# Feed-forward: the output of the second chunk of a half goes in front of the fourth chunk's first layer and the second GELU pair

## The chip, the cores and the metric

The kernel runs on one core of one Trainium2 chip. The time is the device time of one execution in microseconds (us). A core has five engines with an instruction queue each: TensorE (PE, matrix products; its weight loads are shown as PEld), VectorE (DVE), ScalarE (ACT), GpSimd (POOL) and SyncE (SP, which issues transfers). Engines meet through semaphores, and each works through its own queue strictly in order.

## The reference

The input x has the shape (2, 1024, 288), 16 heads of 18. Four layers follow each other. Layers 0 and 1 are quantised transformer blocks; in short:

```python
h = layer_norm(x, ln1_g, ln1_b, 1e-06)
q8, s, sm = quant_act(h)                      # per token: max|h|/127, round, row sum
q, k, v = (quant_linear(q8, s, sm, w, b) for (w, b) in ...)
a8, sa, sma = quant_act(attn(q, k, v))
x = x + quant_linear(a8, sa, sma, wo1, bo1)   # self-attention, 1024 x 1024
...                                           # cross-attention to 154 context tokens, the same way
h = layer_norm(x, ln3_g, ln3_b, 1e-05)
q8, s, sm = quant_act(h)
h = quant_linear(q8, s, sm, wfc1, bfc1)       # 288 -> 1152
h = jax.nn.gelu(h, approximate=False)
q8, s, sm = quant_act(h)
return x + quant_linear(q8, s, sm, wfc2, bfc2)   # 1152 -> 288
```

`quant_act` scales each token by its largest absolute value to integers of at most 127; `quant_linear` multiplies integers by quantised weights and scales back. Layers 2 and 3 are plain cross-attentions to the context, split into 86 text tokens and 68 others, each with its own softmax, without feed-forward. The change touches only the feed-forward, the last block shown.

## The kernel before

x stays in SBUF as 16 chunks of 128 tokens, eight for each of the two batch elements. The work is written as Python generators. `self_attention` is the main one: it runs over four self-attentions (layer 0, batch 0 and 1; layer 1, batch 0 and 1). Beside it, `beside(main, n_main, side, n_side, by)` advances "side" generators in proportion: preparation of weights, the cross-attention and feed-forward of the batch element whose self-attention has ended (`rest`), and the preparation of the next self-attention. So the feed-forward of layer 0, batch 0 runs beside the self-attention of layer 0, batch 1, and so on; the last one, of layer 1, batch 1, runs beside `plain_layers`, layers 2 and 3.

The whole kernel is one block of the Tile scheduler (L53, `schedule_with_timeline_sim=True`). Each engine gets a fixed list of instructions at compile time. The order comes from the order of the program and from a planner's own model of when each instruction would be ready; buffers come from pools with a fixed number of slots, and an instruction that needs a slot waits until its last reader is done. A moved line can therefore change the order of neighbouring work too, of the self-attention as well.

`feed_forward(w, b, name)` (L1313) works in two halves of four chunks; with two layers and two batch elements there are eight halves, called h1 to h8 in order of time. Each half begins with `ln_quantise` (LayerNorm: statistics on DVE L409, normalisation on ACT L422, eight multiplies and adds with gain and bias on POOL L430, then quantisation) and `transposed`. Then a table of (function, chunk) is worked through, and after each entry but `gelu` the generator yields to the main work. The functions are:

- `linear(c)`: the first layer, four times three matmuls (L456, tile `cf`) and a scaling on DVE (L467) into the float tile `ch`, 1152 wide. `ch` has three slots.
- `gelu(c)`: GELU on ACT, in place, for chunk c+1 (L1339) and then chunk c (L1340), tied together by `follow`, so that one load of ACT's function table serves both. The exponentials of the attention (L662) need another table, so a change between the two shows as a table load.
- `integers(c)`: quantises `ch` to the integers `cg`: largest value (DVE L373), scale and reciprocal (DVE L374, L375), small columns on POOL (L1345, L380 to L383), scaling on DVE (L385), rounding with row sum on ACT (L389), two small steps on DVE (L399, L400).
- `output(c)`: two groups of five PE transposes (L1355, `cpt`), each copied by ACT (L1358, `cgT`); ten matmuls (L1361, `co`); a scaling on DVE (L1369, `cu`); the add to x on POOL (L472).

The transposes, the first layer and the output share the two PSUM slots of `mm` (L148). What is called T, O and F with a chunk's number in this text are its transposes, its output matmuls and its first layer. Where a half runs alone it is called bare (h2, h4, h8 around the change); in the others attention work stands between its instructions. Other tiles met below: `aats`, `aatse`, `aato` are scores, exponentials and products of the self-attention (L660, L662, L674), `atse` the same exponentials in the plain layers; `amx` and `amxh` (L600, L607) the search for the largest scores, and `amxsr` (L581) its results on their way.

Of the kernel before, what the change touches and what calls it, by code (L numbers as in the profile page):

```python
# [53 lines left out]
def tile_xattn(ctx: ExitStack, tc: tile.TileContext, ins: dict, out: bass.AP):  # L54
# [56 lines left out]
    def follow(one, other):  # L111

        one, other = (getattr(i, "ins", i) for i in (one, other))
        tc.add_manual_dep(
            one,
            other.name,
            mybir.DependencyInfo(
                mybir.DependencyClass.NoSync, mybir.DependencyReason.DATA
            ),
            reason="kept together",  # L120
        )
# [17 lines left out]
    def big(name):  # L139
        return work.tile([P, FF], F32, tag="big", name=name, bufs=3)  # L140

    def bf(name):
        return work.tile([P, 3 * HQ], BF16, tag="bf", name=name, bufs=3)
# [4 lines left out]
    def mm(name, dtype=F32):  # L148
        n = 512 if dtype == F32 else 1024
        return ps_m.tile([P, n], dtype, tag="mm", name=name)  # L150
# [4 lines left out]
    def view(ap, **kw):  # L155
        names = list(kw)
        return ap.rearrange(f"p ({' '.join(names)}) -> p {' '.join(names)}", **kw)
# [246 lines left out]
    def ln_quantise(c0, ln, eps, s, name, h=None, q=None, eng=nc.gpsimd):  # L404
        st = small.tile([P, HC, 6], F32, tag="bn", name=f"{name}st")
        mv = small.tile([P, HC, 2], F32, tag="mv", name=f"{name}mv")
        rstd = small.tile([P, HC], F32, tag="rstd", name=f"{name}r")
        for c in range(HC):
            nc.vector.bn_stats(st[:, c, :], x[:, c0 + c, :])  # L409
            nc.vector.bn_aggr(mv[:, c, :], st[:, c, :])  # L410
        nc.vector.tensor_scalar(
            rstd, mv[:, :, 1:2].rearrange("p c a -> p (c a)"), eps, None, ALU.add
        )
        nc.gpsimd.tensor_tensor(rstd, rstd, neghalf, ALU.pow)
        shift = small.tile([P, HC], F32, tag="shift", name=f"{name}sh")
        nc.vector.scalar_tensor_tensor(
            shift.unsqueeze(2), mv[:, :, 0:1], -1.0, rstd.unsqueeze(2), ALU.mult, ALU.mult
        )
        if h is None:
            h = view(big(f"{name}h"), c=HC, w=C)  # L420
        for c in range(HC):
            nc.scalar.activation(  # L422
                h[:, c, :],
                x[:, c0 + c, :],
                AF.Identity,
                bias=shift[:, c : c + 1],
                scale=rstd[:, c : c + 1],
            )
            for j, op in ((0, ALU.mult), (1, ALU.add)):
                eng.tensor_tensor(h[:, c, :], h[:, c, :], ln[:, j, :], op)  # L430
        if q is None:
            q = bf(f"{name}q")
        q = view(q[:, 0 : HC * CZ], c=HC, w=CZ)
        quantise(h, q, s, HC, C, f"{name}qs")
        return q

    def transposed(q, name, qT=None):

        if qT is None:
            qT = bf(f"{name}qT")  # L440
        qT = view(qT[:KZ], k=3, t=HQ)
        for c0 in range(0, HC, 2):
            ptv = view(mm(f"{name}pt", BF16)[:KZ, 0 : 6 * P], k=3, t=2 * P)
            for c in range(2):
                for k in range(3):
                    nc.tensor.transpose(
                        ptv[:, k, c * P : (c + 1) * P],
                        q[:, c0 + c, k * KZ : (k + 1) * KZ],
                        ident16,
                    )  # L450
            nc.scalar.copy(qT[:, :, c0 * P : (c0 + 2) * P], ptv)
        return qT
# [5 lines left out]
    def quant_linear(qT, c, w, s, dst, name, shape=lambda ap: ap):  # L458

        qw, row = w  # L460
        ps = mm(name)[:, 0:C]
        matmul3(
            ps,
            lambda k: qT[:, k, c * P : (c + 1) * P],
            lambda k: qw[:, k, :, :],
        )
        nc.vector.scalar_tensor_tensor(  # L467
            dst, shape(ps), s, shape(row), ALU.mult, ALU.mult
        )

    def add_to_x(n, t):
        nc.gpsimd.tensor_tensor(x[:, n, :], x[:, n, :], t, ALU.add)  # L472

    def tmp(name):
        return work.tile([P, C], F32, tag="tmp", name=name, bufs=3)
# [837 lines left out]
    def feed_forward(w, b, name):  # L1313

        qw2, row2 = w["2"]
        for hf in range(2):
            c0 = b * 8 + hf * HC
            s1 = small.tile([P, HC], F32, tag="st", name=f"{name}st")
            q = ln_quantise(c0, w["ln"], 1e-5, s1, f"{name}l")
            yield 8  # L1320
            qT = transposed(q, f"{name}t")
            yield 2
            hs, gs = {}, {}

            def linear(c):
                hs[c] = big(f"{name}h")
                for j, wj in enumerate(w["1"]):
                    quant_linear(
                        qT,
                        c,  # L1330
                        wj,
                        s1[:, c : c + 1],
                        hs[c][:, j * C : (j + 1) * C],
                        f"{name}f",
                    )

            def gelu(c):

                a = nc.scalar.activation(hs[c + 1], hs[c + 1], AF.Gelu)  # L1339
                follow(nc.scalar.activation(hs[c], hs[c], AF.Gelu), a)  # L1340

            def integers(c):
                s = small.tile([P, HC], F32, tag="s", name=f"{name}s")[:, 0:1]
                g = bf(f"{name}g")[:, 0:FZ]
                nc.gpsimd.memset(g[:, FF + NZ : FZ], 0.0)  # L1345
                quantise(hs[c].unsqueeze(1), g.unsqueeze(1), s, 1, FF, f"{name}qs")
                gs[c] = g, s

            def output(c):
                g, s = gs[c]  # L1350
                gT = view(bf(f"{name}gT")[:KF, 0 : 10 * P], k=10, t=P)
                for k0 in (0, 5):
                    ptv = view(mm(f"{name}pt", BF16)[:KF, 0 : 5 * P], k=5, t=P)
                    for k in range(5):
                        nc.tensor.transpose(  # L1355
                            ptv[:, k, :], g[:, (k0 + k) * KF : (k0 + k + 1) * KF], ident16
                        )
                    nc.scalar.copy(gT[:, k0 : k0 + 5, :], ptv)  # L1358
                ps = mm(f"{name}o")[:, 0:C]
                for k in range(10):  # L1360
                    nc.tensor.matmul(  # L1361
                        ps,
                        lhsT=gT[:, k, :],
                        rhs=qw2[:, k, :],
                        start=(k == 0),
                        stop=(k == 9),
                    )
                t = tmp(f"{name}u")
                nc.vector.scalar_tensor_tensor(t, ps, s, row2, ALU.mult, ALU.mult)  # L1369
                add_to_x(c0 + c, t)  # L1370


            for f, c in (
                (linear, 0),
                (linear, 1),
                (gelu, 0),
                (integers, 0),
                (linear, 2),
                (output, 0),
                (integers, 1),  # L1380
                (linear, 3),
                (gelu, 2),
                (output, 1),
                (integers, 2),
                (integers, 3),
                (output, 2),
                (output, 3),
            ):
                f(c)
                if f is not gelu:  # L1390
                    yield 2
# [253 lines left out]
    def rest(n, b, *between):  # L1645
        pre = (L0, L1)[n]
        return chain(
            cross_attention(wb[n], b, f"{pre}b"),
            *between,
            feed_forward(wc[n], b, f"{pre}c"),  # L1650
        )
# [102 lines left out]
```

## Time and profile before

| what | value |
|---|---|
| time, median of three runs (lowest, highest) | 2461.59 us (2456.64, 2463.33) |
| the profiled execution | 2467.29 us, span 2465.5 us |
| granted TensorE clock, mean | 0.871 of full speed |
| busy share: PE, DVE, ACT, POOL | 79%, 72%, 60%, 39% |

The eight halves were found in the trace by their tiles. The page's line of 40 slices for PE and for its clock shows the course:

```profile
PE   2579988888777878887679678877777888778888
PEclk9689999899787989998789689986887988878999
```

One slice is 61.6 us. A digit is the busy share, or the granted clock, in tenths. The feed-forward halves lie around 656 to 767, 1118 to 1231, 1645 to 1755 and 2088 to 2206 us, so in the eleventh to thirteenth slice, the nineteenth and twentieth, the twenty-seventh to twenty-ninth and the thirty-fourth to thirty-sixth (counted from 1): the places with 7, 6 and 7 again belong to them or border on them. In a timeline row the first two numbers are start and length in us, then come engine, line, operation, the tile written and those read, the shape, the number of instructions joined in the row, and in brackets how long the engine had been idle and what released it.

### The profile page before, as it was taken

What the parts mean: (1) busy time and instruction counts of PE and PEld (TensorE: products, weight loads), DVE (VectorE), ACT (ScalarE), POOL (GpSimd) and SP (SyncE); (2) the same over time, 40 slices, a digit from 0 to 9 for tenths busy, and PEclk for the clock granted to TensorE, in tenths of its full rate; (3) what the DMA queues carried; (4) which work ended last, traced back from release to release, by engine and by line L of the source; (5) the groups of instructions that cost most, each with busy time, mean ns of one, the idle gap of its engine ahead of it and who ended that gap; (6) DMA issues with size and microseconds to landing.
All of it is one profiled execution on the core that took longest, in us unless ns stands there. A gap on an engine that the chain in (4) does not pass through costs nothing. (4 is left out here: it accounts for less than half of the span.)

```text
span 2465.5 us, 33556 instructions
## 1 busy us (share of the span) xinstructions
PE 1941.7 (79%) x10524; PEld 852.0 (35%) x10524; DVE 1777.5 (72%) x4213; ACT 1475.3 (60%) x2897; POOL 973.6 (39%) x2038
## 2 busy tenths in 40 slices
PE   2579988888777878887679678877777888778888
PEld 1223333332233243323333243323334443444444
DVE  6699997699775758997469848883255785745666
ACT  3257767675577667756676357756555665554443
POOL 4334224551325455432353545523247562313320
PEclk9689999899787989998789689986887988878999
DMA  3523212221001322100032031100123311112321
GB/s 76 169 69 98 68 40 65 69 64 42 9 1 52 108 76 61 48 24 13 12 101 79 23 90 47 38 9 12 35 73 92 86 55 31 50 38 74 85 79 38
DMA packets 160003, 141.58 MB, mean 57 GB/s; under 512 B 44123, under 2 KB 156339, under 8 KB 159760
## 3 DMA queue, kind: packets, MB, share of 16 engines
q1 hardware_dynamic: 148656, 121.90, 17.0%
q0 software_dynamic: 3584, 12.04, 2.0%
q10 hardware_dynamic: 7584, 5.47, 1.2%
q8 instruction: 84, 1.38, 0.2%
q14 instruction: 95, 0.78, 0.1%
HBM read 96.60 MB, written 39.37 MB: 55 GB/s over the span
## 5 line engine op out<-in xcount | busy, mean ns | idle before, releaser
L662 ACT ACTIVATE L_xattn_aatse<-L_xattn_aats 128x512 f32<-128x512 f32 x1024 | 575.9, 597 | 267.5 <-PE L_xattn_aats L660 253.0
L607 DVE TENSOR_REDUCE L_xattn_amxh<-L_xattn_amx 128x1 f32<-128x512 f32 x1024 | 658.5, 680 | 71.6 <-PE L_xattn_amx L600 68.7
L660 PE MATMUL L_xattn_aats<-L_xattn_aqT,kT 120*128 120x512 bf16 x1024 | 389.3, 406 | 88.8 <-ACT L_xattn_aatse L662 46.5
L600 PE MATMUL L_xattn_amx<-kT,L_xattn_aqT 108*128 108x512 bf16 x1024 | 388.1, 414 | 65.5 <-DVE L_xattn_amxh L607 40.3
L674 PE MATMUL L_xattn_aato<-L_xattn_aatse,L_xattn_av 128*32 128x512 f32 x2048 | 297.7, 652 | 43.5 <-ACT L_xattn_aatse L662 40.1
L641 POOL TENSOR_TENSOR L_xattn_bmxm<-L_xattn_bmxm,L_xattn_bm 128x308 f32<-128x308 f32 x256 | 199.7, 785 | 161.1 <-ACT L_xattn_bmxm L640 152.4
L662 ACT ACTIVATE L_xattn_atse<-L_xattn_ats 86x512 f32<-86x512 f32 (+1 forms) x256 | 142.2, 590 | 118.3 <-PE L_xattn_ats L660 99.7
L660 PEld LDWEIGHTS <-kT 120*128 120x128 bf16 x1024 | 96.2, 101 | 329.6 <-issue 292.1
L600 PEld LDWEIGHTS <-L_xattn_aqT 108*128 108x128 bf16 x1024 | 102.7, 103 | 216.3 <-issue 162.3
L646 DVE TENSOR_REDUCE L_xattn_mxn<-L_xattn_mx 128x2 f32<-128x172 f32 (+1 forms) x512 | 124.6, 303 | 39.2 <-PE L_xattn_mx L630 38.4
L640 ACT COPY L_xattn_bmxm<-L_xattn_bmx 128x308 f32<-128x308 f32 x256 | 104.0, 416 | 69.4 <-DVE L_xattn_bmxn L646 30.1
L646 DVE TENSOR_REDUCE L_xattn_bmxn<-L_xattn_bmxm 128x2 f32<-128x308 f32 x256 | 116.5, 460 | 25.2 <-POOL L_xattn_bmxm L641 24.9
L747 ACT ACTIVATE L_xattn_batse<-L_xattn_batse 128x512 f32<-128x512 f32 x160 | 100.2, 630 | 41.4 <-DVE L_xattn_batse L746 37.9
L660 PE MATMUL L_xattn_ats<-L_xattn_qT,L_xattn_kT 120*86 120x512 bf16 (+1 forms) x256 | 100.1, 422 | 29.9 <-ACT L_xattn_atse L662 15.5
L746 DVE TENSOR_TENSOR L_xattn_batse<-L_xattn_bats,L_xattn_bmT 128x512 f32<-128x512 f32 x160 | 107.7, 681 | 21.3 <-PE L_xattn_bats L752 8.0
L1495 PE MATMUL L_xattn_o<-wo,L_xattn_p 128*128 128x288 f32 x320 | 99.9, 455 | 9.6 <-DVE L_xattn_p L819 9.3
L674 PEld LDWEIGHTS L_xattn_aato<-L_xattn_aatse,L_xattn_av 128*32 128x32 f32 x2048 | 42.3, 111 | 172.3 <-ACT L_xattn_aatse L662 143.2
L630 PE MATMUL L_xattn_bmx<-L_xattn_bkT,L_xattn_bqT 108*128 108x154 bf16 x512 | 73.8, 245 | 23.8 <-DMA L_xattn_bqT<-L_xattn_bqr 8.8
L630 PE MATMUL L_xattn_mx<-L_xattn_kT,L_xattn_qT 108*128 108x154 bf16 x512 | 71.5, 257 | 22.3 <-DMA L_xattn_qT<-L_xattn_r 7.5
L1361 PE MATMUL L_xattn_co<-L_xattn_wfc2t,L_xattn_cgT 117*128 117x288 bf16 x320 | 65.9, 360 | 26.8 <-ACT L_xattn_cgT L1358 25.4
L674 PE MATMUL L_xattn_ato<-L_xattn_atse,L_xattn_v 68*32 68x512 f32 (+1 forms) x512 | 77.4, 677 | 8.1 <-DVE L_xattn_atT L847 4.3
L1495 PEld LDWEIGHTS L_xattn_o<-wo,L_xattn_p 128*128 128x128 f32 x320 | 65.9, 214 | 34.2 <-DVE L_xattn_p L819 14.8
(632 smaller groups left out, 3768.0 us busy)
## 6 DMA issues: line engine op xcount, KB each, us to landing
kT<-L_xattn_akr SPq DMA_DIRECT2D x192, 72.0 KB
L_xattn_aqT<-L_xattn_aqr SPq DMA_DIRECT2D x192, 72.0 KB
L_xattn_bqT<-L_xattn_bqr SPq DMA_DIRECT2D x192, 72.0 KB
L_xattn_qT<-L_xattn_r SPq DMA_DIRECT2D x192, 72.0 KB
L_xattn_akr<-L_xattn_akst SPq DMA_DIRECT2D x16, 324.0 KB
L_xattn_aqr<-L_xattn_aqst SPq DMA_DIRECT2D x16, 324.0 KB
L_xattn_bqr<-L_xattn_bqst SPq DMA_DIRECT2D x16, 324.0 KB
L_xattn_r<-L_xattn_qst SPq DMA_DIRECT2D x16, 324.0 KB
```

The lines of the kernel that those rows point to most:

```text
L600: nc.tensor.matmul(sp, lhsT=qt[:KR, j, c * P : (c + 1) * P], rhs=kt[:KR, j, a * 512 : (a + 1) * 512], start=True, stop=True,)
L607: nc.vector.tensor_reduce(halves[:, a, c, j, :], sp, AX.X, ALU.max, negate=True)
L630: nc.tensor.matmul(sp[:, j * T : (j + 1) * T], lhsT=qt[:KR, 2 * a + j, c * P : (c + 1) * P], rhs=kt[:KR, 4 * g + 2 * a + j, 0:T], start=Tr ...
L640: nc.scalar.copy(lm, of)
L641: nc.gpsimd.tensor_tensor(lm, lm, mask[:, c : c + 1, 0:T].to_broadcast([P, 2, T]), ALU.add)
L646: nc.vector.tensor_reduce(nm[:, c, 2 * a : 2 * a + 2, n], of[:, :, k0:k1], AX.X, ALU.max, negate=True,)
L660: nc.tensor.matmul(sp, lhsT=keys(j), rhs=qt[:KM, j, :], start=True, stop=True)
L662: nc.scalar.activation(e, sp, AF.Exp)
L674: made = nc.tensor.matmul(po[32 * i : 32 * i + 32, :], lhsT=lhsT, rhs=rhs, start=start, stop=stop)
L746: nc.vector.tensor_tensor(e, sp, maskT[:, m, :], ALU.add)
L747: nc.scalar.activation(e, e, AF.Exp)
L1495: nc.tensor.matmul(ps, lhsT=t[:, c * P : (c + 1) * P], rhs=wo[:, u0 + u, :], start=(u == 0), stop=(u == len(tiles) - 1),)
```

## The change

One entry of the table in `feed_forward` moves up by two places. The output of chunk 1 (its transposes, copies, matmuls, scaling and add to x) is handed to the scheduler directly behind the integers of chunk 1, and so in front of chunk 3's first layer and of the GELU of chunks 3 and 2; before, it came behind both. The generator yields at the same number of places; one yield that came behind chunk 1's output now comes before chunk 3's first layer. No instruction is added or taken away in the program, no buffer changes.

```diff
@@ -1378,9 +1378,9 @@
                 (linear, 2),
                 (output, 0),
                 (integers, 1),
+                (output, 1),
                 (linear, 3),
                 (gelu, 2),
-                (output, 1),
                 (integers, 2),
                 (integers, 3),
                 (output, 2),
```

In the compiled lists of instructions the change shows in all eight halves, and around them in the order of attention work too: the lists of the engines are the same up to about 680 us of the old time line and from about 2190 us on. The lists of PE, DVE, POOL and SP hold the same instructions as before in another order; that of ACT holds two table loads fewer.

## The prediction

> **What bounds the kernel now.** I read the page's busy shares first, then the eight stretches in which a feed-forward half runs, then the timeline of one half, then the list of waits. (1) Over the whole span no engine is full: PE 79%, DVE 72%.
>
> ```profile
> PE 1941.7 (79%) x10524; PEld 852.0 (35%) x10524; DVE 1777.5 (72%) x4213; ACT 1475.3 (60%) x2897; POOL 973.6 (39%) x2038
> ```
>
> (2) Windows: us, then the busy time of PE, weight load, DVE, ACT and POOL, then the granted clock. In order: a stretch between feed-forwards, the second halves of layer 0's two batch elements (h2, h4), and the first half of layer 1 (h5).
>
> ```profile
> 830.00:900.00 70.00, 58.16 (x324) 24.54 (x324) 56.22 (x130) 45.88 (x106) 32.42 (x68) 0.93 0.23 64
> 720.00:767.00 47.00, 29.77 (x190) 16.52 (x188) 26.02 (x66) 31.76 (x52) 16.33 (x37) 0.78 0.03 8
> 1190.00:1231.00 41.00, 22.56 (x133) 12.71 (x131) 21.27 (x54) 25.94 (x42) 14.29 (x34) 0.71 0.05 14
> 1645.00:1702.00 57.00, 42.57 (x238) 19.21 (x235) 28.13 (x66) 40.60 (x67) 23.48 (x60) 0.73 0.05 12
> ```
>
> PE falls from 83% to 63% and 55%: in these halves a chain bounds, which hops from engine to engine. (3) The chain of h2, from the timeline (start, length, engine, line, tiles, in brackets the idle time before and its releaser):
>
> ```profile
> 738.23 1.32 PE L1355 MATMUL L_xattn_cpt<-ident,L_xattn_cg 128*117 128x128 bf16 x10 [1.95 <-ACT L_xattn_cg L389]
> 739.85 2.58 PE L1361 MATMUL L_xattn_co<-L_xattn_wfc2t,L_xattn_cgT 117*128 117x288 bf16 x10 [0.31 <-ACT L_xattn_cgT L1358]
> 745.39 0.52 DVE L467 SCALAR_TENSOR_TENSOR L_xattn_ch<-L_xattn_cf,L_xattn_cst,L_xattn_wfc_864row 128x288 f32<-128x288 f32 x1
> 745.79 0.69 ACT L1358 COPY L_xattn_cgT<-L_xattn_cpt 117x640 bf16<-117x640 bf16 x1 [1.95 <-PE L_xattn_cpt L1355]
> 746.50 1.28 ACT L1339 ACT_TABLE_LOAD   x1
> 746.54 0.79 PE L1361 MATMUL L_xattn_co<-L_xattn_wfc2t,L_xattn_cgT 117*128 117x288 bf16 x5
> 747.80 1.16 ACT L1339 ACTIVATE L_xattn_ch<-L_xattn_ch 128x1152 f32<-128x1152 f32 x1
> 750.05 2.61 DVE L373 TENSOR_REDUCE L_xattn_cqs<-L_xattn_ch 128x1 f32<-128x1152 f32 x2 [4.13 <-ACT L_xattn_ch L1340]
> 750.65 1.38 PE L1361 MATMUL L_xattn_co<-L_xattn_wfc2t,L_xattn_cgT 117*128 117x288 bf16 x5 [3.32 <-ACT L_xattn_cgT L1358]
> 753.84 0.51 DVE L1369 SCALAR_TENSOR_TENSOR L_xattn_cu<-L_xattn_co,L_xattn_cs,L_xattn_wfc2row 128x288 f32<-128x288 f32 x1
> 757.26 1.52 PE L1355 MATMUL L_xattn_cpt<-ident,L_xattn_cg 128*117 128x128 bf16 x10 [5.24 <-ACT L_xattn_cg L389]
> ```
>
> The reader is to see two things. After chunk 3's first layer the half is one chain: GELU pair, two reduces, scale, rounding, transposes of chunk 2 at 757.26. And chunk 1's output (745.32 to 752.03 on PE) lies inside that chain's shadow: PE waits 3.32 us in it, and then 5.24 us more, and nobody needs it.
>
> **The change, part by part.** The order of instructions shows the same work on PE, DVE, POOL and the queues; ACT loses two table loads. In all eight halves ten transposes (T1), two copies, ten matmuls (O1), the scaling `cu` on DVE and the add to x on POOL move in front of chunk 3's first layer (F3) and the GELU pair.
>
> *T1 and O1 ahead of F3.* They leave their cover and F3 comes later by what they take on PE. Lower bound, all rows at the full clock: 0.44+0.44 transposes, 0.69 copy (the second beside it), 0.79+0.79 matmuls = 3.15. Upper bound, chunk 0's own pass: 742.43−738.23 = 4.20. I take 3.4, nearer the first, since PE's row there is warm (granted 0.88 from 742.2 to 746). F3 itself took 742.43 to 745.91 = 3.48, bound by its DVE rows. So in h2 F3's end goes to 742.43+3.4+3.48 = 749.3. Cheaper than 3.4, because before GELU waited for the load and for chunk 1's first copy: it began at 747.80, 1.9 us behind F3. Now the table is held in h2, and GELU begins at 749.3: **+1.5**. In h4 and h8 (GELU at 1211.90 and 2184.63 before) the same sum gives +1.4 and +1.5, if the load is early there too.
>
> *What comes back.* `cu` leaves the DVE chain between reduces and scale: −0.42 in h2 (753.84 to the next row at 754.26), −0.43 and a 0.44 statistics step in h4, −0.48 in h8 (2189.47 to 2189.95). Bare halves: h2 +1.1, h4 +0.5, h8 +1.1.
>
> *Mixed halves (h1, h3, h5, h6, h7), where a self- or cross-attention shares the engines.* GELU moves by +2.6 (h1, h3), +3.3 (h5), +2.8 (h6), +2.1 (h7): F3's delay of 3.4 less what GELU waited for its load. In h7 the attention's exponentials stand behind the pair:
>
> ```profile
> 2121.88 1.28 ACT L1339 ACT_TABLE_LOAD   x1
> 2123.17 1.16 ACT L1339 ACTIVATE L_xattn_ch<-L_xattn_ch 128x1152 f32<-128x1152 f32 x1
> 2127.53 1.28 ACT L662 ACT_TABLE_LOAD   x1 [1.68 <-issue]
> 2128.82 1.08 ACT L662 ACTIVATE L_xattn_atse<-L_xattn_ats 86x512 f32<-86x512 f32 x2
> ```
>
> so both streams are late: +2.0. In h1 and h3 the exponentials lose 0.4, the rounding 1.6: +1.5 each. In h5 POOL's casts, not GELU, release chunk 3's last transpose (1.79 us of PE at 1691.59), and the Wq and Wk issues and 13 casts of L106 (0.27 us each) now run ahead of them: +1.0. In h6 +0.9. Bounds: 0 if the attention's work fills every delay, the GELU shift itself if it fills nothing; I take the values given, because exponentials wait in the same ACT queue.
>
> *Table loads.* One pair fewer: three exponentials go ahead of h2's first pair. They cost 1.1 of ACT less in h2's front and are charged in h1's end: −1.1. The rows price a load at 1.28, GELU starting 0.02 behind; the pair is 2.57, already in the +1.5 of h2 (one) and hidden in ACT's free 32% of h2 (the other). [...]
>
> *Waits that stand elsewhere now.* PE: O1 waits for chunk 1's copies (0.69) with F3 queued behind it, and GELU behind F3; that is in the 3.4. DVE: `cu` waits for O1 in front of F3's scalings, which could not run before O1's end anyway: nothing. ACT: the next LN's normalisation (L422, 2.18 us at 741.67) comes behind both copies, at about 744.6 to 746.8; POOL, its reader, is busy until 747.2 with what follows, so nothing; uncovered it would be those 2.9. SP: the feed-forward issues no transfer; in h1 and h3 the maxima's copy (L581, 0.56) and its transfer go ahead of the second pair instead of behind, 0.56 on GELU, within the +2.6.
>
> *POOL.* Chunk 1's add moves in front of the next LN's eight multiplies and adds (L430; "multiplies" below), which wait there for `cu`. In h2 O1 ends at 745.83; `cu` to first multiply took 1.39 for chunk 0 (742.43 to 743.82), so multiplies run 747.22 to 753.3 instead of 743.82 to 749.94. Their reader, the LN's reduce, stood at 752.58 and moves with GELU to 754.1. Hidden, by 0.8; costed at nothing, 1.9 us per half if that cover is gone.
>
> *Knock-on.* Between the halves the planner orders attention work anew (776–900, 939–1068, 1236–1373, 1722–1842, 1907–2029 us; at most 68 places on PE). No row prices it. Bounds ±5 from the largest piece that I could follow (the L240 preparation of wo, and one 7.11 us idle of the maxima behind the keys); I take 0.
>
> Sum: 1.5+1.1+1.5+0.5+1.0+0.9+2.0+1.1−1.1 = **+8.5**. The profiled execution took 2467.29 (span 2465.5 and 1.8 around it): 2475.8. It lies 5.7 above the median, above every shown run; on the median 2461.59 the sum gives 2470.1.
>
> [...]
>
> **The rivals.** *Cover lost* (the forecast): +1.6 (mixed halves all hidden: h4 and h8 only) to +14.9 (4.2 instead of 3.4 in eight halves): 2463 to 2476.5; 2470.
>
> *The stall goes, and that is what counts (faster).* Place: O1's second five matmuls behind GELU.
>
> ```profile
> PE L_xattn_co L1361 <- ACT L_xattn_cgT L1358: 25.4, 22, 3.3
> ```
>
> Four waits of 3.32 stand in h2, h4, h5, h8. In h5 the attention's products queue behind it on PE, in h6 the second five follow the first only at 1739.65, 4.57 after 1735.08. If attention work fills F3's delay there and PE goes on at once: −3.3−4.6 = −7.9, 2453.7; with all four stalls 13.3, 2448.3. It decides where attention work is ready at the moved place; against it, three of the four stalls are in bare halves, where PE then idles anyway.
>
> *POOL becomes late (slower still).* If LN multiplies already bound the reduce, 1.9 in six halves: 8.5+11.4 = 19.9, 2481.5. It needs a slack below 1.9 before; h2 had 752.58−749.94 = 2.64, h4 2.74, which speaks against it.
>
> *Nothing*: F3's delay and regained DVE steps cancel, ±2: 2462.
>
> **How the numbers follow.** A measurement of this kernel can tell about 0.3%, 7.4 us, from no change. Cover lost .55 (its range straddles 2469: slower .38, same .17); stall .27 (faster .25, same .02); POOL .10 (slower); nothing .08 (same). Faster .25, same .27, slower .48. Low end: the stall rival at its most, 2448.3, less the 2.57 of a pair of loads, 2446. High end: 2481.5, which POOL and cover lost with the knock-on's 5 both reach, and 1.7 for the spread above the median (2463.33−2461.59): 2483. Cases of both signs hold chance; the forecast's own range is 2463 to 2476.5.
>
> **What would show it.** Right: in h2 no ACT table load ahead of the second pair, first GELU near 749.3, second five of O1 without the 3.32 idle, T2 near 758.4 with an idle of about 9 us before it; in h7 exponentials near 2131; two table loads fewer. Wrong: T2 in h2 before 757.5, LN multiplies releasing the reduce (POOL), or the span changing more outside the feed-forward stretches than in them, which would put the planner's new order, costed at nothing, in first place.

## The result, and the profile after

The changed kernel took 2493.3 us (median of four runs, 2492.07 to 2502.65) beside 2459.2 us of the kernel before on the same chip (four runs, 2456.64 to 2463.33): ratio 1.0145, 95% interval 1.0115 to 1.0175, so about 34 to 36 us more. The forecast was slower, at 2470 (range 2446 to 2483): the direction was right, the size was a quarter of what came, and the time lies above the range. The profiled execution after took 2494.28 us with a span of 2492.5 us.

The page after, first the busy shares:

```profile
PE 1953.1 (78%) x10524; PEld 852.0 (34%) x10524; DVE 1781.6 (71%) x4213; ACT 1476.9 (59%) x2895; POOL 977.2 (39%) x2038
```

The work is the same (ACT two instructions fewer, the two table loads). PE is busy for 11 us longer with the same 10524 matmuls, at a granted clock of 0.86 after and 0.871 before; the other engines' busy time grows by 2 to 4 us. The windows that answer to the four shown of before (us, then the busy time of PE, weight load, DVE, ACT and POOL, then the granted clock):

```profile
839.00:909.00 70.00, 56.19 (x305) 23.38 (x306) 56.57 (x124) 43.32 (x96) 30.61 (x61) 0.91 0.23 61
729.00:776.00 47.00, 28.22 (x179) 16.65 (x177) 25.86 (x66) 27.46 (x46) 16.48 (x37) 0.72 0.03 8
1212.00:1253.00 41.00, 24.31 (x136) 11.99 (x135) 21.19 (x52) 27.53 (x44) 14.62 (x34) 0.69 0.04 10
1670.00:1727.00 57.00, 39.35 (x234) 18.55 (x233) 28.21 (x66) 40.82 (x67) 23.48 (x60) 0.78 0.05 12
```

The three halves look as before. In the stretch between (first line) TensorE gets 305 matmuls done in 70 us where it got 324 before: less is done there in the same time.

The timeline of half 2 after (start, length, engine, line, tiles; in brackets the idle time before and its releaser):

```profile
746.69 1.32 PE L1355 MATMUL L_xattn_cpt<-ident,L_xattn_cg 128*117 128x128 bf16 x10 [6.00 <-ACT L_xattn_cg L389]
748.32 2.58 PE L1361 MATMUL L_xattn_co<-L_xattn_wfc2t,L_xattn_cgT 117*128 117x288 bf16 x10 [0.31 <-ACT L_xattn_cgT L1358]
750.69 1.51 PE L1355 MATMUL L_xattn_cpt<-ident,L_xattn_cg 128*117 128x128 bf16 x10
752.27 1.67 PE L1361 MATMUL L_xattn_co<-L_xattn_wfc2t,L_xattn_cgT 117*128 117x288 bf16 x10
755.33 6.05 POOL L430 TENSOR_TENSOR L_xattn_alh<-L_xattn_alh,L_xattn_ln 128x288 f32<-128x288 f32 x8
756.42 0.49 DVE L467 SCALAR_TENSOR_TENSOR L_xattn_ch<-L_xattn_cf,L_xattn_cst,L_xattn_wfc_864row 128x288 f32<-128x288 f32 x1
756.94 1.16 ACT L1339 ACTIVATE L_xattn_ch<-L_xattn_ch 128x1152 f32<-128x1152 f32 x1 [1.94 <-DVE L_xattn_ch L467]
761.78 1.34 DVE L373 TENSOR_REDUCE L_xattn_alqs<-L_xattn_alh 128x4 f32<-128x1152 f32 x1
765.61 1.32 PE L1355 MATMUL L_xattn_cpt<-ident,L_xattn_cg 128*117 128x128 bf16 x10 [9.40 <-ACT L_xattn_cg L389]
```

The change did what it says. Chunk 1's transposes and output (750.69 to 753.94) stand in front of chunk 3's first layer, no table load stands in front of the second GELU pair, the wait of 3.32 us is gone, and PE's idle time in front of chunk 2's transposes is one piece of 9.40 us. Yet these transposes come 18.92 us after chunk 0's (746.69 to 765.61), and they came 19.03 after before: this half lost nothing.

So the time went elsewhere. Taking the same VectorE instruction in both traces, the 27 us between the two spans come about like this: 6.8 stand at 677 us already, where the lists of the two kernels are still the same (the last section comes back to this); 8.2 are added inside the four pairs of halves, 12.8 between 769 and 1121 us, where no feed-forward runs, 5.0 in the other stretches between, and 5.7 are given back at the end, behind 2194 us, where the lists are the same again. In the stretches between, the planner had put attention work in another order. The experiments separate that order from the moved output.

### The profile page after: what moved, and what is told of

It reads as the page before. It is cut to its first block, busy times and chain, and to the rows that moved or that the text cites. A ratio compares the mean times of both kernels' runs of the same rounds, so it can differ in the third digit from the quotient of the medians.

```text
span 2492.5 us, 33583 instructions
## 1 busy us (share of the span) xinstructions
PE 1953.1 (78%) x10524; PEld 852.0 (34%) x10524; DVE 1781.6 (71%) x4213; ACT 1476.9 (59%) x2895; POOL 977.2 (39%) x2038
## 5 line engine op out<-in xcount | busy, mean ns | idle before, releaser
L660 PE MATMUL L_xattn_aats<-L_xattn_aqT,kT 120*128 120x512 bf16 x1024 | 394.6, 414 | 95.5 <-ACT L_xattn_aatse L662 55.1
L600 PE MATMUL L_xattn_amx<-kT,L_xattn_aqT 108*128 108x512 bf16 x1024 | 396.1, 422 | 65.0 <-DVE L_xattn_amxh L607 40.1
L646 DVE TENSOR_REDUCE L_xattn_bmxn<-L_xattn_bmxm 128x2 f32<-128x308 f32 x256 | 116.5, 461 | 29.3 <-POOL L_xattn_bmxm L641 29.0
L746 DVE TENSOR_TENSOR L_xattn_batse<-L_xattn_bats,L_xattn_bmT 128x512 f32<-128x512 f32 x160 | 107.4, 681 | 27.8 <-PE L_xattn_bats L752 10.2
L630 PEld LDWEIGHTS <-L_xattn_bqT 108*128 108x128 bf16 x512 | 47.0, 105 | 80.7 <-issue 50.0
```

Of the source, the lines that this page charges most:

```text
L600: nc.tensor.matmul(sp, lhsT=qt[:KR, j, c * P : (c + 1) * P], rhs=kt[:KR, j, a * 512 : (a + 1) * 512], start=True, stop=True,)
L630: nc.tensor.matmul(sp[:, j * T : (j + 1) * T], lhsT=qt[:KR, 2 * a + j, c * P : (c + 1) * P], rhs=kt[:KR, 4 * g + 2 * a + j, 0:T], start=Tr ...
L646: nc.vector.tensor_reduce(nm[:, c, 2 * a : 2 * a + 2, n], of[:, :, k0:k1], AX.X, ALU.max, negate=True,)
L660: nc.tensor.matmul(sp, lhsT=keys(j), rhs=qt[:KM, j, :], start=True, stop=True)
L746: nc.vector.tensor_tensor(e, sp, maskT[:, m, :], ALU.add)
```

## The experiments

**How an order is held.** At the end of the program an edge without a wait was added from each instruction of an engine to the next one in a written list, so the compiler issues them in that list's order and the planner decides nothing:

```diff
     beside(plain, 128, last, 216, 96)
     drain(plain)
+    for engine, packed in _ORDER.items():
+        traced = [...]                      # this engine's instructions as traced
+        kept = [traced[i + d] for i, d in enumerate(moves)]
+        for one, other in zip(kept[1:], kept):
+            tc.add_manual_dep(one, other.name, ... NoSync ..., reason="order kept")
+_ORDER = {...}                              # the lists, packed
```

The traces show that the lists then stand as written: in e5, for one, TensorE, VectorE, ScalarE and GpSimd work in the order of before up to 930 us and from 1121 us on, and in the order of after in between. The lists of the two kernels hold the same instructions up to many points of time, so one can be taken up to such a point and the other from there on. Each ratio compares with runs of the kernel before that were taken beside it; their medians were 2467.1 us (e1 to e4), 2464.9 (e5 to e8), 2458.6 (e9 to e12) and 2467.2 (e13, e14).

**e1 to e4: inside the halves or between them.** Edit of e1: the program after, order of after in the four feed-forward stretches, of before elsewhere. Edit of e2 to e4: the program before, order of after only between the stretches (e3 the first of three, e4 the other two).

> The changed program, with every engine's list held to a written order: the order after the change in the four stretches of feed-forward (680 to 770, 1118 to 1233, 1640 to 1757 and 2060 to 2206 us of the old time line), the order before the change everywhere else. Theory (the planner's new order of the attention work between the halves costs most): about 7 us over before, 2466, as the terms of my sum inside the halves have it (8.5). Rival (the moved output itself costs it, through waits that I did not see): the whole 34 us, 2493. Rival (only both together cost): no more than 3 us over before.

> The program of before, held to the order after the change between the feed-forward stretches only (770 to 1118, 1233 to 1640, 1757 to 2060 us); inside the stretches nothing moves, so the change itself is undone. Theory (new order of the attention work): about 20 us over before, 2480. Rival (the moved output itself): within 3 us of before. Rival (only both together): within 3 us of before as well, with e1 small too.

> As e2, but only the first of the three stretches between (770 to 1118 us) has the order after the change. Theory: about 12 us over before, 2471, since the delay of the changed kernel's trace against the old one grows by some 12 us there. Rivals: within 3 us of before.

> As e2, but only the second and third stretches between (1233 to 1640 and 1757 to 2060 us). Theory: about 8 us over before, 2467: the delay grows by 3 to 4 us in the second stretch and 4 to 5 us in the third. Rivals: within 3 us of before.

Measured: e1 ratio 1.0005 (0.9978 to 1.0032), e2 1.0105 (1.0066 to 1.0143), e3 1.0043 (1.0023 to 1.0063), e4 1.0063 (1.0033 to 1.0092). In us of 2467: +1, +26, +11, +16. The whole change, with the attention work held to its old order, costs nothing that can be told from zero. The new order of the attention work costs 26 us although chunk 1's output stands where it stood. The two parts of it add up (11 + 16); the second is twice the 8 that I had expected, with an interval from 8 to 23. The rival that the moved output itself costs the 34 us has fallen, and so has the one that only both together cost.

**Stretch by stretch.** Each held kernel repeats an order exactly, so the traces can be pooled. The table takes the same VectorE instruction at each border in every trace, and gives the mean length in us of a stretch over the traces that have the order of before in it, and over those that have the order of after (in brackets smallest and largest, and how many traces were taken):

| stretch (old time line) | order of before | order of after | difference |
|---|---|---|---|
| 677 to 769, h1 and h2 | 90.5 (90.0 to 91.2, 10) | 93.4 (93.2 to 93.7, 3) | +2.9 |
| 769 to 930 | 162.0 (161.4 to 164.4, 10) | 165.4 (164.6 to 165.9, 4) | +3.4 |
| 930 to 1121 | 191.6 (190.3 to 192.8, 7) | 198.2 (196.7 to 199.6, 5) | +6.6 |
| 1121 to 1234, h3 and h4 | 113.7 (112.9 to 114.3, 9) | 114.3 (114.2 to 114.4, 2) | +0.6 |
| 1234 to 1430 | 194.4 (191.2 to 197.4, 9) | 197.1 (196.8 to 197.5, 3) | +2.7 |
| 1430 to 1644 | 215.2 (211.3 to 218.7, 11) | 215.5 (214.6 to 216.6, 3) | +0.3 |
| 1644 to 1757, h5 and h6 | 112.7 (112.1 to 114.3, 8) | 115.6 (114.7 to 116.5, 2) | +2.9 |
| 1757 to 1901 | 139.5 (136.2 to 144.3, 8) | 143.2 (141.9 to 144.5, 3) | +3.7 |
| 1901 to 2060 | 157.2 (155.2 to 159.1, 8) | 165.9 (163.1 to 167.9, 3) | +8.6 |
| 2060 to 2194, h7 and h8 | 136.9 (134.5 to 139.2, 8) | 136.3 (135.2 to 137.4, 2) | −0.6 |

Inside the halves: +5.8. Between them: +25.3, of which 15.2 lie in two stretches, 930 to 1121 and 1901 to 2060. Those of 1234 to 1430 and of 1757 to 1901 overlap with the spread of the old order. The sum, 31, lies inside the interval of the whole change (28 to 43 us).

**e5, e9, e13, e14: where in 930 to 1121.** Edit of e5: as e2, order of after from 930 to 1118 only. e13 and e14 split that at 1001. e9 is e5 with three places mended by hand:

```diff
 VectorE's list, first place (the second and third alike)
-L746 batse      # idle 1.34 in front of it, waiting for bats
 L607 amxh
 L607 amxh
+L746 batse
 TensorE's list
-L674 bats x4
 L600 amx x2
+L674 bats x4
```

> The program of before; only from 930 to 1118 us of the old time line every engine's list has the order after the change. Theory (one place of the first stretch between is bad, in which VectorE is nearly full and waits more often at the head of its queue): 6 to 8 of the 10.7 us of e3, 2474 beside a before of 2467. Rival (the loss is spread evenly over the re-ordered stretch): half, about 5 us. Rival (it comes from 770 to 930, where the weights are prepared in another order): within 2 us of before.

> The kernel of e5 with three places mended by hand: where VectorE stood longest at the head of its queue before a mask addition of the cross-attention (L746, idle 1.34, 2.02 and 2.07 us in the trace of e5), the addition goes behind the next two to four reductions (L607, L646, L781), and on TensorE the scores that it reads go behind the next two to four matmuls. Theory (the loss of 930 to 1118 us is VectorE idle, put there by the order): the stretch from 930 to 1121 us, 197.2 us in the trace of e5 and 190.7 to 192.8 in the traces with the old order, falls by 2 to 5 us; the whole is 2 to 5 us below e5's 7 over before. Rival (the waits only show a delay whose cause is elsewhere, and come back behind the next instruction): the stretch stays within 1 us of 197.2.

> As e5, but only from 930 to 1001 us has the order after the change. In the trace of e5 the delay grows to 4 us by 1009 us and is back at 0.6 at 1033. Theory (a delay inside the stretch is given back where VectorE has work in store; only idle time that is still there when VectorE runs without a gap, from 1016 us on, counts): the stretch from 930 to 1121 stays within 2 us of the old 191.6 (seven traces, 190.3 to 192.8). Rival (the first waits already cost): 195 to 196.

> As e5, but only from 1001 to 1121 us has the order after the change. Theory: nearly all of e5's loss, the stretch from 930 to 1121 takes 195 to 198 us, and VectorE is idle for 4 us or more of it above the old 17. Rival (the first waits already cost): 191 to 193.5.

Measured: e5 1.0029 (1.0005 to 1.0052), 7 us; e9 1.0037 (1.0023 to 1.0051); e13 1.0001 (0.9977 to 1.0024); e14 1.0011 (0.9987 to 1.0035). The times of e13 and e14 do not tell them from before; the stretch in their traces does. The windows from border to border (us, then the busy time of PE, weight load, DVE, ACT and POOL, then the granted clock), of the kernel before:

```profile
930.17:1120.91 190.74, 160.81 (x917) 59.48 (x911) 173.74 (x373) 126.33 (x268) 85.12 (x186) 0.95 0.15 40
```

of e1, old order here:

```profile
936.24:1128.88 192.64, 162.16 (x917) 59.87 (x910) 174.04 (x373) 126.61 (x268) 85.28 (x186) 0.94 0.15 39
```

of e2, new order:

```profile
939.51:1138.52 199.01, 165.61 (x918) 61.87 (x911) 175.04 (x373) 126.82 (x268) 85.00 (x182) 0.91 0.14 38
```

of e9:

```profile
931.13:1133.67 202.54, 168.39 (x918) 61.62 (x911) 175.72 (x373) 126.35 (x268) 84.21 (x182) 0.90 0.13 37
```

of e13:

```profile
937.97:1132.51 194.54, 162.13 (x917) 60.59 (x910) 172.61 (x373) 127.07 (x268) 84.59 (x186) 0.95 0.14 39
```

and of e14:

```profile
939.95:1138.61 198.66, 165.13 (x918) 60.89 (x914) 175.47 (x371) 126.71 (x268) 85.37 (x182) 0.91 0.14 38
```

VectorE is busy for 91% of this stretch in the old order (173.74 of 190.74) and does the same work in every kernel. Its idle time (the sum of the gaps in front of its instructions) is 17.1 us in the mean of the seven old traces and 23.4 in the five new ones: 6.3 of the 6.6 us. From 1901 to 2060 it is 37.1 and 43.3, 6.2 of 8.6. That alone does not single VectorE out, since an engine with the same work in a longer stretch must be idle for longer: ScalarE's idle time grows by as much, from 65.1 to 71.3 and from 60.3 to 67.3. TensorE is the exception. It is busy for longer over the same matmuls, 165.6 instead of 161.6 in the first stretch and 138.4 instead of 131.0 in the second, where it, and not VectorE (121), is the fullest engine; the last section gives its clock. What VectorE waits for in 930 to 1121, before and in e2, from the list of waits (us in total, times, longest):

```profile
DVE L_xattn_amxh L607 <- PE L_xattn_amx L600: 6.6, 10, 1.9
DVE L_xattn_bmxn L646 <- POOL L_xattn_bmxm L641: 3.9, 7, 1.5
DVE L_xattn_batse L746 <- PE L_xattn_bats L674: 1.3, 3, 0.7
```

```profile
DVE L_xattn_batse L746 <- PE L_xattn_bats L674: 6.4, 6, 2.1
DVE L_xattn_amxh L607 <- PE L_xattn_amx L600: 6.3, 10, 1.5
DVE L_xattn_bmxn L646 <- POOL L_xattn_bmxm L641: 5.3, 7, 1.4
```

The mask additions of the cross-attention (L746) now wait at the head of VectorE's queue for scores that TensorE has not made. But that is where the loss shows, not what could be taken out singly: e9 moved three such waits (5.4 us of idle) behind work that looked ready, and the stretch grew from 197.2 to 202.5 instead of falling. The theory of e9 fell, and its rival (the stretch stays) fell too. This is one trace each: TensorE was busy for 168.4 us in it beside 164.1 in e5's, at a clock of 0.90 beside 0.92, and the times of the two kernels (+9 and +7) do not tell them apart. Two of the three places also lie in front of 1001 us. e13 and e14, again by one trace each, give the place: the part behind 1001 us alone costs 198.7 − 191.6 = 7.1 us, as much as the whole, about as expected (195 to 198 for the stretch); the part in front alone costs 2.9, which I had expected to be given back and which was not in e13. The two do not add up to e5's 5.6: behind the new early part the new late part costs less. So most of the loss comes with the order behind 1001 us. Which of its moved places decides it, and whether it costs time through VectorE's waits, stays open. Holding one engine alone to the new order wasn't tried, since the lists of one stretch depend on each other.

**e6, e7, e10, e11, e12: is it the moved work or any cause.** None of these holds an order; the planner orders everything. e6 adds one memset of six columns in the first half:

```diff
                 nc.gpsimd.memset(g[:, FF + NZ : FZ], 0.0)
+                if (name, b, hf, c) == ("L0_xattn_c", 0, 0, 0):
+                    nc.gpsimd.memset(g[:, FF + NZ : FZ], 0.0)
```

e7, e10, e11 and e12 make the change in some halves only (here e7: the first half; the others with b and the layer alone):

```diff
                 (integers, 1),
+                *([(output, 1)] if (name, b, hf) == ("L0_xattn_c", 0, 0) else []),
                 (linear, 3),
                 (gelu, 2),
-                (output, 1),
+                *([] if (name, b, hf) == ("L0_xattn_c", 0, 0) else [(output, 1)]),
```

> The program of before with one added memset of six zero columns on GpSimd, in the first chunk of the first half, a repetition of the one at L1345; nothing is moved by hand and no order is held. About 1100 lines of VectorE's list of 3429 rows stand elsewhere then. Theory (what the changed kernel lost is the planner's new order, which any small cause brings about): a change of 5 us or more in either direction although the added work is 0.1 us. Rival (the planner's order only gets worse because the output was moved): within 3 us of before.

> Chunk 1's output is moved in the first of the eight halves only, no order held. Direct cost by my sum 1.5 us. Theory (planner's new order): another 5 us or more in either direction, since the lists of all engines differ up to the end. Rival (cost in proportion to the moved work): 34/8, about 4 us over before.

> Chunk 1's output is moved in the two halves of layer 0's first batch element only, no order held. Theory: directly 1.5 us by my sum, 2.7 by the trace of e1; with the planner's new order of all that follows 5 us or more over before, most of it between 930 and 1121 and between 1757 and 2060 us. Rival (cost in proportion to the moved work): a quarter of the whole, 7 to 9 us, inside 676 to 769 us.

> The same in the two halves of layer 0's second batch element only. Theory: directly 2.0 us by my sum, 0.5 by the trace of e1, nothing before 1121 us; what the planner's new order adds lies behind 1234 us and is 5 us or more. Rival (in proportion to the moved work): 7 to 9 us, inside 1121 to 1234 us.

> The same in the last two halves only, where hardly anything is left for the planner to order anew behind them. Theory: directly 3.1 us by my sum, 0.2 by the trace of e1; within 5 us of before. Rival (in proportion to the moved work): 7 to 9 us.

Measured: e6 1.0002 (0.9976 to 1.0028), e7 1.0034 (1.0011 to 1.0056), e10 1.0038 (1.0019 to 1.0058), e11 1.0040 (1.0024 to 1.0057), e12 0.9989 (0.9974 to 1.0005). In us: 0, +8, +9, +10, −3.

e10 is the clearest: it moves work in h1 and h2 only, and its lists from 769 to 1121 us are those of the full change, with the same cost there (165.8 and 196.7 us, in the table). It then goes its own way and gets some of it back (108.5 from 1644 to 1757, where the old order has 112.7). e11 leaves everything up to 1121 as it was, its own halves take 112.9 (old order 113.7), and its 10 us come behind: 162.7 from 1901 to 2060 against 157.2. In both the cost is not where the moved work is; the rivals 'in proportion, inside its own stretch' have fallen for these two, though their totals of 7 to 9 us were near. e7 alone does not decide: 8 us, from 3 to 14, holds its rival's 4 as well. e12, with little left to order anew, cost nothing, against its rival's 7 to 9.

e6 tests nothing, because the new order that I expected of it does not show in its trace. TensorE, VectorE and ScalarE do the same operations on the same tiles and shapes as before, row by row (10524, 4213 and 2897 of them), and so does GpSimd but for the added memset; only an exchange between two instructions of the same tiles and shape would not show. Its stretches (135.8 from 1757 to 1901, 156.6 from 1901 to 2060) are then further samples of the old order; with them, no difference in the table changes by more than 0.4. Every run in which the planner did re-order the attention work (e7, e10, e11 and the whole change) lost time. Whether an order that the planner makes for some other cause would lose it as well was not tried.

**e8: what the wait of 3.32 us is worth.** Lists of before, but chunk 1's second copy (L1358) goes in front of the GELU pair on ScalarE in the five halves where it stood behind:

```diff
 ScalarE's list, five halves
 L1358 cgT       # first copy
+L1358 cgT       # second copy
 L1339 ch        # table load, GELU of chunk 3
 L1340 ch        # GELU of chunk 2
-L1358 cgT
```

> The program of before, every list held to the order of before, but in the five halves where chunk 1's second copy (L1358) stands behind the GELU pair on ScalarE it stands in front of it. The wait of 3.32 us of TensorE in front of the second five output matmuls goes; the GELU pair starts some 0.7 us later. Theory (that wait lies in the shadow of the GELU chain): 2 to 4 us over before, five times 0.7. Rival (the wait counts, as my rival 'the stall goes' had it): 5 to 8 us under before.

Measured: 1.0014 (0.9995 to 1.0032), +3 us. TensorE's wait for these copies fell as in the changed kernel. The list of waits before (us in total, times, longest):

```profile
PE L_xattn_co L1361 <- ACT L_xattn_cgT L1358: 25.4, 22, 3.3
```

and in e8:

```profile
PE L_xattn_co L1361 <- ACT L_xattn_cgT L1358: 12.4, 18, 1.9
```

13 us less of waiting, no time gained: the stall lay in the shadow of the GELU chain.

## Why the prediction was right or wrong

**T1 and O1 ahead of F3: right, a little dear.** Taken at 3.4; after, from O0's end at 750.90 to O1's end at 753.94 it is 3.04, just under the lower bound of 3.15. GELU in h2 begins 10.25 us after T0, before 9.57: +0.7 where I had +1.5, since F3 also took 3.14 instead of 3.48 (753.77 to 756.91) and began just before O1's end. In h4 GELU begins 6.40 after O0's end (1228.61 to 1235.01), before 5.01 (1206.89 to 1211.90): +1.4, as worked out.

**What comes back: right in h4, more in h2.** Counted from O0's end, T2 is later by 0.7 in h4 (forecast +0.5) and earlier by 0.1 in h2 (forecast +1.1).

**Mixed halves: the sum about right, single terms not.** Pair by pair the forecast was 1.5 (h1+h2), 2.0 (h3+h4), 1.9 (h5+h6) and 3.1 (h7+h8), together 8.5; the table has 2.9, 0.6, 2.9 and −0.6, together 5.8. That the sum comes near is luck in part: the pairs miss by +1.4, −1.4, +1.0 and −3.7, which partly cancel. h7 was the worst: I said that both streams are late there because the exponentials stand behind the pair. The rows after (ScalarE, timeline):

```profile
2155.84 1.28 ACT L1339 ACT_TABLE_LOAD   x1
2157.13 1.16 ACT L1339 ACTIVATE L_xattn_ch<-L_xattn_ch 128x1152 f32<-128x1152 f32 x1
2158.20 1.15 ACT L1340 ACTIVATE L_xattn_ch<-L_xattn_ch 128x1152 f32<-128x1152 f32 x1
2159.37 1.28 ACT L662 ACT_TABLE_LOAD   x1
2160.66 1.08 ACT L662 ACTIVATE L_xattn_atse<-L_xattn_ats 86x512 f32<-86x512 f32 x2
```

From GELU to the exponentials it is 3.53 us now and was 5.65: the copy that stood between them (L581) went ahead of the pair, and the 1.68 us of idle time closed. That took the delay up. I had counted such a copy for h1 and h3 only, and only its price in front of GELU.

**Table loads and POOL: right in kind.** Two loads fewer; what they are worth (−1.1 in the sum) no run separates. In h2 the multiplies end at 761.38 and their reader starts at 761.78: hidden by 0.4 (I had 0.8), so the rival 'POOL becomes late' did not come. In h7 a load takes 1.28 and GELU begins 0.01 after it ends (2157.12), beside the 0.02 that the prediction read from h2.

**The rival 'the stall goes': wrong,** by e8: no gain when the wait is taken away by itself.

**The gap of 9 us and the clock: the gap came (9.40 in h2), and the sum has no term for it.** In h2, T2 after the gap took 1.32 us for ten transposes and O2 2.58, at a granted clock of 0.50 (765.6 to 770.0); before, after 5.24 us of idle time, they took 1.52 and 2.58, at 0.50 as well (757.3 to 761.7): the longer gap cost nothing there.

**The step that failed is 'Knock-on':** "No row prices it. Bounds ±5 from the largest piece that I could follow … I take 0." It is worth 25.3 us, four times the part that I worked out in detail, and it alone puts the time above the range. Three things were wrong in it. The bounds came from the two pieces that I had followed, not from the size of what was re-ordered: the stretches 769 to 1121, 1234 to 1430 and 1757 to 2060 are some 850 us long, and 25 us are 3% of that. I took the middle between gain and loss. And the prediction read the load of the stretches between from shares over the whole span, in which no engine is full, and from one window (830 to 900); from 930 to 1121 VectorE is busy for 91%, which leaves a delay less room to be caught up. Why the new order is slower, by VectorE's waits, by TensorE's lower clock or by something else, stays open. The sentence on what would make the prediction wrong ("the span changing more outside the feed-forward stretches than in them") named the case that came.

## What to carry to other kernels

Where a planner orders the instructions, an edit has two prices: its own, and that of the order that the planner makes of everything behind it. Hold the order and time the edit, then hold the edit away and time the order: here the first cost 6 us by the traces (1 by the times, at most 8) and the second 26. Before blaming or praising an edit, look for the stretches whose lists changed, compare their lengths under the old and the new order, and do not bound the unknown by the pieces that were easy to follow.

## What the runs showed of the hardware

Up to about 660 us the lists of all sixteen profiled kernels are the same, and yet they reach the table's first border between 677.5 and 687.2 us. Between the traces of before and after, three of the steps (near 325, 357 and 417 us) are places where TensorE ran slower in the profiled execution of after: it was granted 0.58 from 326.1 to 330.2, 0.54 from 360.6 to 364.0 and 0.50 from 422.2 to 425.2 us, where before had 1.00, 1.00 and 0.97 at the same instructions. The same six matmuls, 1.69 us at 0.97 in the timeline of before:

```profile
417.24 1.69 PE L456 MATMUL L_xattn_bcvp<-L_xattn_wv,ctxT 96*128 96x288 f32 x6 [2.42 <-DVE L_xattn_bcky L513]
```

and 3.22 us at 0.50 in that of after:

```profile
422.21 3.22 PE L456 MATMUL L_xattn_bcvp<-L_xattn_wv,ctxT 96*128 96x288 f32 x6 [2.52 <-DVE L_xattn_bcky L513]
```

So the place at which TensorE ran slower differs from one execution to the other, with steps of 1.3 to 1.6 us; what decides the place no run here shows. Two single profiles can thus lie 10 us apart with the same lists up to there (before and e14 reach the border at 930 us at 930.17 and 939.95 us), and only stretches pooled over several traces, or several rounds of times, carry differences of a few us. In the two costly stretches the granted clock also fell with the new order. From 930 to 1121 us it lay between 0.94 and 0.95 in the seven old traces and between 0.90 and 0.92 in the five new ones; from 1901 to 2060 between 0.88 and 0.92 in the old ones and between 0.85 and 0.87 in the new. Whether that follows from the waits or brings them about was not separated. Two figures speak against the clock as the whole cause. e13 kept a clock of 0.95 and yet took 194.5 us, 2.9 more than the old mean. And from 1901 to 2060 a straight line through the old traces, e6 among them (159.0 us at 0.88, 155.2 at 0.92 at the ends), gives by estimate some 2.4 us for the fall of the mean clock from 0.900 to 0.863, of a difference of 8.6.
